# The third graph layer, too, does its first 256 destinations by fetching the rows of single edges

## The chip, the cores and the metric

The kernel runs on one core of a Trainium2 chip. The metric is the device time of one execution in microseconds. Before the change, three timed executions gave 1886.87, 1888.71 and 1895.72 us; the median is 1888.71 us.

## The reference: what is computed

There are 3125 nodes with 256 features each, and 103125 edges (50000 random pairs in both directions and one loop per node), sorted by destination. Four blocks follow each other, each with a layer norm ahead of it and a residual sum behind it: a graph attention network of three layers, a mixture of 16 experts (two per node), a graph sum layer, and a mixture of 8 experts (one per node). The change concerns the three attention layers, and the way in which the rows of the third go on to the 16 experts:

```
def _gat_layer(x, src, dst, W, al, ar, b, n_nodes):
    h = x @ W
    el = h @ al
    er = h @ ar
    e = jax.nn.leaky_relu(el[src] + er[dst], 0.2)
    m = jax.ops.segment_max(e, dst, num_segments=n_nodes)
    ex = jnp.exp(e - m[dst])
    s = jax.ops.segment_sum(ex, dst, num_segments=n_nodes)
    alpha = ex / s[dst]
    return jax.ops.segment_sum(alpha[:, None] * h[src], dst, num_segments=n_nodes) + b

h = relu(_gat_layer(layernorm(x), src, dst, W1, al1, ar1, b1, n))
h = relu(_gat_layer(h, src, dst, W2, al2, ar2, b2, n))
x = x + _gat_layer(h, src, dst, W3, al3, ar3, b3, n)
```

## The kernel before

**Tiles and groups.** Nodes lie in 25 tiles of 128 (the last has 53). Destinations are done in 13 groups: twelve of 256 (two tiles) and one of 53. A matrix of edge counts, source by destination, is kept on the chip as bytes; the first layer builds it on the way. The exponential of the leaky score is written as a product and a maximum, so that a group needs, for each of the 25 source tiles (a *step*), one DVE instruction and two products on PE. The DVE instruction (L1388) makes `pm` = max(tau, rho) x counts, 128 sources by 256 destinations. The products (L1391) multiply its two halves with the sources' rows `h` (256 features and a column of weights, 257 columns) and accumulate in PSUM. A float32 product stands in the profile as two records, so a step has four and a group 100. Six `pm` buffers let DVE run ahead of PE. `terms` (L1277, L1280) makes tau of the next group in the middle of a group.

**What follows a group.** During the next group, `divide` (L1428 to L1437) divides by the weights and adds the bias. In layers one and two, the "onward" steps then turn the tile (L1289), multiply it with the next layer's weights (L1161) and keep rows, scores and exponentials (L1168 to L1172). In layer three, the router takes over (`Router.group`): `norm` (L616 to L621), `gate` (L629 to L639), and `send` (L241 to L249 and L644 to L677). `send` picks two experts per node, finds each row's place by a running count `pre` (PE at L661 and L662) and scatters two rows per node to HBM with an indirect DMA on POOL's queue (L677), four per group. POOL also adds the bias to the residual input `y` (L1359) and writes node numbers and weights into the rows (L675, L676).

**The rows apart (class `Apart`).** In layer two, the first four tiles (512 destinations) are not done by products. As layer one ends, every source row with its weights (258 numbers) is saved to HBM by a DMA on SP's queue. In layer two POOL then fetches single rows by indirect DMA (L1933), one destination per partition: 38 edges for each tile (`OWN`), and beforehand 20 more (`HEAVY`) for the at most 128 destinations of all four tiles that have more than 38 edges. Each fetch of 128 rows is one *slot*. Four slots make a batch, and five batches of buffers make a ring. DVE makes the coefficients of a batch (`apart_co`, L1950) and adds up each slot (`apart_acc`, L1957 and L1959). The sums of the heavy destinations are brought back to their places by a product with a transposed one-hot matrix (L1964; the matrix is made in `begin`, L1875 to L1914). `EVERY`, `LANDED` and `STEP` say after how many steps of the layer each batch, slot and fetch stands in the program; a fetch into the ring stands behind the last slot of the batch whose buffer it takes.

**What sets the order.** Layer two is issued as written (`manual_schedule`). Layers one and three are ordered by the scheduler of the tile framework, which places instructions by its own estimates. Each engine works through its queue in order, so an instruction that waits holds all those behind it. In layer two, ten groups (2 to 11) and the short last one are left. In layer three, all 13 are done by products, and the first of them starts its sources at tile 4, since the tiles done apart come last (`of`).

**The write of empty rows.** `spare_rows` clears parts of the HBM buffers by 34 DMAs on SP's queue, one in every eighth step from the third group of layer one on.

Of the kernel before, what the change touches and what calls it, by code (L numbers as in the profile page):

```python
# [10 lines left out]
F32 = mybir.dt.float32  # L11
# [6 lines left out]
OP = mybir.AluOpType  # L18
# [4 lines left out]
P = 128  # L23
# [543 lines left out]
class Router:  # L567
# [6 lines left out]
    def __init__(self, tc, cp, ident, eps, iota, count, rows, sums, gate_w, gate_b, table):  # L574
# [3 lines left out]
        self.before, self.every = count  # L578
        self.gw = cp.tile([P, KD, NX0], F32, name="gate_w")
# [25 lines left out]
    def group(self, wp, rp, pp, x, t0, n):  # L605
# [35 lines left out]
        def send():  # L641
# [16 lines left out]
            for i, t in enumerate(tiles):  # L658
                nc.vector.tensor_tensor(self.pre[:, t + 1], self.pre[:, t], sel[:, i], op=OP.add)
            rank = pp.tile([P, n, NX0], F32, name="ps_z")  # L660
            nc.tensor.matmul(rank, self.before, sel, start=True, stop=False)  # L661
            nc.tensor.matmul(rank, self.every, self.pre[:, t0:t0 + n], start=False, stop=True)  # L662
# [420 lines left out]
APART = 2  # L1083
FEW = 2 * APART
OWN = 38
HEAVY = 20
SLOTS_OF = [(FEW, HEAVY)] + [(t, OWN) for t in range(FEW)]
BATCH_OF = 4
BATCHES_OF = [(t, k, min(BATCH_OF, n - k)) for t, n in SLOTS_OF for k in range(0, n, BATCH_OF)]
RING = 5  # L1090
LANDED = 19.0
FETCH = 11
BEGIN = 0
RANK = [(5, 0), (5, 4), (5, 6), (5, 9), (5, 14), (5, 17), (6, 8)]
EVERY = 1.31
STEP, LAST_STEP = 0.976, 0.25
# [78 lines left out]
def dense_attention(tc, dram, counts, x_in, big, ident, eps, layers, src, dst, rows, high, make_router, over, count):  # L1175
# [10 lines left out]
    with tc.tile_pool(name="dw", bufs=1) as cp, tc.tile_pool(name="dwl", bufs=2) as wl, \  # L1186
# [3 lines left out]
        with tc.tile_pool(name="dp", bufs=6) as pmp, tc.tile_pool(name="ds", bufs=2) as sp, \  # L1190
# [92 lines left out]
            def onward_steps(at, y, t, r, name, nxt, w, save):  # L1283
# [15 lines left out]
                def keep():  # L1299
                    nxt.keep(t, r, held["ps"])  # L1300
                    if save:
                        save.save(nxt, t, r)
# [6 lines left out]
            raws, soon = [None], []  # L1309
            fills = []  # L1310
            for i in range(3):
                last = i == 2
                bt_i = bt
                if last:
# [6 lines left out]
                    nxt, we_n = None, None  # L1321
                else:
                    nxt = Sources(tc, big, small)
                    we_n, bt, products = attention_weights(tc, wl, cp, layers, i + 1, now.rho[:, NT - 1:])
                    products()
                apart_now, now_apart = i == 1, []
                if apart_now:
                    hold = ExitStack()
                    hp = hold.enter_context(tc.tile_pool(name="hp", bufs=1))
                    raws[0] = hp  # L1330
                    hq = hold.enter_context(tc.tile_pool(name="hq", bufs=1, space=PSUM))
                    def finished(t, acc, b=bt_i, nxt=nxt, w=we_n):
                        col = hp.tile([P, 1], F32, name="apart_col", bufs=2)
                        nc.vector.tensor_scalar(col, acc[:, D:], 1e-30, None, op0=OP.max)
                        nc.vector.reciprocal(col, col)
                        nc.vector.scalar_tensor_tensor(acc[:, :D], acc[:, :D], col, b, op0=OP.mult, op1=OP.add)
# [5 lines left out]
                if apart_now:  # L1342
                    order.enter_context(tc.manual_schedule())
# [788 lines left out]
```

## Time and profile before the change

| what | value |
|---|---|
| timed runs, median (lowest to highest) | 1888.71 us (1886.87 to 1895.72) |
| the profiled execution, its own time | 1840.01 us |
| its span, first to last instruction | 1838.2 us |
| mean granted clock of PE | 0.990 |
| layer one, first to last product L1391 | 67.8 to 443.8 us |
| layer two | about 453 to 726 us |
| layer three | about 727 to 1021 us |
| from the end of layer three to the first expert's products | 1021 to 1042.9 us |

The profile has a page of totals and groups of instructions ("line engine op, out<-in xcount | busy us, mean ns | idle before, and what ended it"), a list of waits ("who waited for whom: us in total, times, longest"), busy times by window, and timelines ("start, length, engine, line, operation; in brackets the idle time just before it and what ended it"). Line numbers are those of the kernel before. A busy PE says little on its own, since products overlap; the pace of its records and what it waits for say more. Lengths on DVE overlap too: two of them in a row can start closer together than one of them lasts.

### The profile page before, as it was taken

The page shows a single profiled execution, that of the slowest core. Times are in us where ns is not written, and L with a number is a line of the kernel's source. Part 1 is how long each engine was busy: PE and PEld are TensorE (multiplying, and loading weights), DVE is VectorE, ACT ScalarE, POOL GpSimd, SP SyncE. Part 2 cuts the span into 40 slices and gives each one's busy share as a digit, 9 for nine tenths or more (in the row PEclk, how much of TensorE's full clock was granted, in tenths as well). Part 3 has the DMA queues.
Part 4 walks back from the last instruction along what each step waited for, and adds up shares of the span by engine and source line. Part 5 has one row for each costly group of instructions (what it writes and reads, how often), then busy time and mean ns, then how long its engine had stood idle before and what let it go on. Part 6 is the DMA issues. An engine that isn't in the chain of part 4 may idle for free. (4 is left out here: it accounts for less than half of the span.)

```text
span 1838.2 us, 27323 instructions
## 1 busy us (share of the span) xinstructions
PE 1771.2 (96%) x9249; PEld 1389.5 (76%) x9249; DVE 1017.4 (55%) x2865; ACT 725.4 (39%) x2078; POOL 501.5 (27%) x636
## 2 busy tenths in 40 slices
PE   5999999999999999999999799999989999999997
PEld 4788888887887886888888466666668886555886
DVE  6888888875777887777777422222262222233221
ACT  3767667671111111222222211111148998444221
POOL 5210110000677774223322233333200000222221
PEclk9999999999999999999999899999999999999999
DMA  4111213757333332211111576776330002624664
GB/s 118 33 48 47 67 64 139 298 236 312 80 93 95 98 93 78 62 46 40 40 44 37 178 196 196 204 217 168 66 82 1 1 1 74 225 115 166 215 203 127
DMA packets 118370, 211.50 MB, mean 115 GB/s; under 512 B 14843, under 2 KB 80929, under 8 KB 118184
## 3 DMA queue, kind: packets, MB, share of 16 engines
q1 hardware_dynamic: 78228, 130.30, 20.9%
q0 software_dynamic: 24848, 56.84, 11.8%
q10 hardware_dynamic: 15138, 22.44, 3.7%
q8 instruction: 79, 1.29, 0.3%
q14 instruction: 77, 0.63, 0.1%
HBM read 118.61 MB, written 93.00 MB: 115 GB/s over the span
## 5 line engine op out<-in xcount | busy, mean ns | idle before, releaser
L1391 PE MATMUL acc<-big,pm 128*128 128x257 f32 x3400 | 787.7, 383 | 8.9 <-DVE pm L1388 8.9
L1391 PEld LDWEIGHTS acc<-big,pm 128*128 128x128 f32 x3400 | 628.6, 190 | 99.4 <-DVE pm L1388 15.4
L1388 DVE SCALAR_TENSOR_TENSOR pm<-tau,big,counts 128x256 f32<-128x256 f32 x850 | 398.3, 487 | 99.9 <-PE acc L1391 96.0
L1933 POOL DMA_INDIRECT apart_row<-apart_rows,apart_who x172 | 186.7, 1085 | 62.6 <-issue 39.3
L775 PE MATMUL ps_h<-xsT,w 128*128 128x384 f32 x512 | 168.4, 487 | 0.6 <-ACT xsT L751 0.6
L1543 PE MATMUL acc<-msg,cr 128*128 128x512 f32 (+1 forms) x625 | 157.9, 403 | 0.0
L775 PEld LDWEIGHTS ps_h<-xsT,w 128*128 128x128 f32 x512 | 96.7, 190 | 66.9 <-issue 1.9
L1543 PEld LDWEIGHTS acc<-msg,cr 128*128 128x128 f32 (+1 forms) x625 | 114.7, 185 | 29.2 <-ACT cr L1539 1.2
L1539 ACT ACTIVATE cr<-counts 128x256 fp32r<-128x256 uint8 (+1 forms) x325 | 130.6, 402 | 14.2 <-PE acc L1543 7.0
L1799 ACT CAST counts<-acc_c 128x500 uint8<-128x500 f32 (+1 forms) x155 | 95.9, 677 | 94.8 <-PE acc_c L1789 94.7
L1024 PE MATMUL ps_y<-t_wd,hsT 128*128 x480 | 108.8, 380 | 0.4 <-ACT hsT L1052 0.4
L1774 DVE TENSOR_TENSOR ohk<-iota_k,key 128x2016 f16<-128x2016 f16 (+1 forms) x79 | 94.6, 1197 | 19.8 <-PE acc_c L1789 19.7
L778 ACT ACTIVATE silu<-ps_h 128x384 f32<-128x384 f32 x64 | 31.4, 490 | 182.2 <-PE ps_h L775 182.1
L795 POOL DMA_INDIRECT sums<-y,who x48 | 74.7, 1556 | 85.9 <-DVE y L793 73.0
L1024 PEld LDWEIGHTS ps_y<-t_wd,hsT 128*128 128x128 f32 x480 | 88.8, 190 | 11.6 <-ACT hsT L1052 0.6
L779 DVE TENSOR_TENSOR hid<-silu,ps_h 128x384 f32<-128x384 f32 x64 | 35.2, 553 | 108.7 <-PE ps_h L775 103.9
L1768 ACT ACTIVATE ohs<-iota_s,low 128x128 f16<-128x128 f16 x286 | 94.1, 400 | 0.0
L930 PE MATMUL ps_H<-big,t_w 128*128 128x512 f32 (+1 forms) x224 | 93.1, 552 | 0.8 <-ACT H L932 0.5
L790 PE MATMUL ps_o<-w,hid 128*128 128x256 f32 x384 | 87.2, 379 | 0.0
L1789 PEld LDWEIGHTS <-ohs 128*128 128x128 f16 x1250 | 77.7, 98 | 10.9
L1789 PE MATMUL acc_c<-ohk,ohs 128*128 128x125 f16 x1250 | 84.5, 218 | 0.0
L1959 DVE SCALAR_TENSOR_TENSOR apart_acc<-apart_row,apart_co,apart_acc 128x257 f32<-128x257 f32 x167 | 80.9, 485 | 1.6
(380 smaller groups left out, 2073.5 us busy)
## 6 DMA issues: line engine op xcount, KB each, us to landing
rows<-empty SPq DMA_DIRECT2D x16, 2564.0 KB, 15.7
w<-in_L_ffn_w_dram ACTq DMA_DIRECT2D x42, 512.0 KB, 4.9
hs<-rows SPq DMA_DIRECT2D x29, 641.0 KB, 4.4
big<-in_L_ffn_w_dram SPq DMA_DIRECT2D x30, 512.0 KB, 9.2
rows<-empty SPq DMA_DIRECT2D x16, 516.0 KB, 4.8
t_wd<-in_L_ffn_Wd_dram SPq DMA_DIRECT2D x8, 1024.0 KB, 10.7
xs<-rows SPq DMA_DIRECT2D x15, 387.0 KB, 3.4
bias<-in_L_ffn_bd_dram SPq DMA_DIRECT2D x30, 128.0 KB, 4.0
```

Of the source, the lines that this page charges most:

```text
L775: nc.tensor.matmul(ps, w[:, k, j * P:(j + 1) * P], xsT[:, k], start=(k == 0), stop=(k == KD - 1))
L930: nc.tensor.matmul(ps[:, :n], a[:, k, j * P:(j + 1) * P], xnT[:, k, c:c + n], start=(k == 0), stop=(k == KD - 1))
L1024: nc.tensor.matmul(ps, hsT[:, j], d[:, ds(e, 1), j, :].rearrange("p o f -> p (o f)"), start=(j == 0), stop=(j == nh - 1))
L1388: nc.vector.scalar_tensor_tensor(pm[:, :n], tau[:, :n], now.rho[:, of:of + 1], edges[:, of, :n], op0=OP.max, op1=OP.mult)
L1391: nc.tensor.matmul(acc[:r, j, :D + 1], pm[:, q:q + r], now.h[:, of, :D + 1], start=(s == 0), stop=(s == NT - 1))
L1539: nc.scalar.activation(cr[:, :n], edges[:, s, :n], AF.Copy, accum_out=seen[:, a * NT + s:a * NT + s + 1])
L1543: nc.tensor.matmul(acc[:r, j].rearrange("p h d -> p (h d)"), cr[:, q:q + r], msg[:, s].rearrange("p h d -> p (h d)"), start=(s == 0), stop ...
L1768: nc.scalar.activation(far[:, i], self.iota_s, AF.Abs, scale=-1.0, bias=self.low32[:, batch, i:i + 1])
L1774: nc.vector.tensor_tensor(to[:, i:tiles].rearrange("p t (x u) -> p t x u", u=2), iota.rearrange("p (x u) -> p x u", u=2)[:, None].to_broad ...
L1789: nc.tensor.matmul(acc[:, u], ohs[:, i], ohk[:, i, :KEYS], start=(t == 0), stop=(t == TW - 1))
L1799: nc.scalar.copy(to[:, :, d0 % PAIR:d0 % PAIR + whole * WIN].rearrange("p s (u d) -> p u s d", u=whole), acc[:, :whole])
L1933: nc.gpsimd.indirect_dma_start(out=row[:, j], out_offset=None, in_=self.table[:, :], in_offset=bass.IndirectOffsetOnAxis(ap=self.who[:, q ...
```

## The change

- `SKIP = [0, 2, 1]`: layer two skips its first two groups as before, and layer three now skips its first group (tiles 0 and 1), which is done by row fetches: 20 heavy slots and 2 x 38, 96 in all, in 25 batches.
- As layer two goes on, its rows are saved to a second table in HBM.
- The ring of layer three has three batches; its slots are planned from 22 us on, one in every 1.9 steps (`EVERY`), against 1.31 us in layer two. What both layers need (row numbers, the transposed one-hot matrix, which slots are real) is kept over both (`stay`).
- Layer three is still ordered by the scheduler, but `pinned` fixes the order of all `pm`, `apart_co` and `apart_acc` instructions on DVE among themselves, as written. The product that brings back the heavy sums takes its PSUM tile from the common pool `ps_m` (two buffers) and holds it until its tile is done.
- The residual input of tiles 0 and 1 is loaded into `y_out` directly; when tile 1 is done, its routing is put into the current group's steps 15, 17 and 20 (or the next group's). The running count `pre` goes by the order of sending (`sent`) and no longer by tile number.
- `begin` moves from step 0 to step 11, just ahead of the first fetches, in both layers.
- After the last group of layer two, the onward steps come five steps earlier, as they did after layer one.
- The writes of empty rows come in every sixth step; their buffer lies in memory that layer one gives back.

```diff
--- before.py
+++ after.py
@@ Router.send
-            for i, t in enumerate(tiles):
-                nc.vector.tensor_tensor(self.pre[:, t + 1], self.pre[:, t], sel[:, i], op=OP.add)
+            k = self.sent
+            self.sent += n
+            for i in range(n):
+                nc.vector.tensor_tensor(self.pre[:, k + i + 1], self.pre[:, k + i], sel[:, i], op=OP.add)
...
@@ constants
-APART = 2
-FEW = 2 * APART
+SKIP = [0, 2, 1]
+FEW = 4
-RING = 5
-LANDED = 19.0
-BEGIN = 0
-EVERY = 1.31
-STEP, LAST_STEP = 0.976, 0.25
+RING = [0, 5, 3]
+LANDED = [0.0, 19.0, 22.0]
+EVERY = [0.0, 1.31, 1.9]
+STEP = [0.0, 0.976, 1.0]
+LAST_STEP = 0.25
@@ dense_attention
-                apart_now, now_apart = i == 1, []
+                apart_now, now_apart, fixed = SKIP[i] > 0, [], i == 1
+                if apart_now and not stays:
+                    stays.append(tc.tile_pool(name="hk", bufs=1))
+                    apart.stay(third.enter_context(stays[0]), pp)
...
+                    if fixed:
+                        hq = hold.enter_context(tc.tile_pool(name="hq", bufs=1, space=PSUM))
+
+                    def finished(t, acc, b=bt_i, nxt=nxt, w=we_n, i=i, hp=hp):
                         col = hp.tile([P, 1], F32, name="apart_col", bufs=2)
...
+                        to, add = (acc[:, :D], b) if i < 2 else (y_out[:, t], y_out[:, t])
+                        apart.pinned(lambda: nc.vector.scalar_tensor_tensor(to, acc[:, :D], col, add, op0=OP.mult,
+                                                                            op1=OP.add))
+                        if i < 2:
+                            soon.extend(onward_steps(now_step[0] + 1, lambda: acc, t, P, "yT1", nxt, w,
+                                                     lambda *of: apart.save(of[0], i + 1, *of[1:])))
+                        elif t % 2:
+                            steps = router.group(wp, rp, zp, y_out, t - 1, 2)
+                            start = now_step[0] + 1
+                            start += max(0, 15 - start % NT) if start % NT < 18 else NT + 15 - start % NT
+                            soon.extend(zip((start, start + 2, start + 5), steps))
+
+                    now_apart += apart.events(i, hq, finished)
+                    if last:
+                        for t in range(2 * SKIP[i]):
+                            nc.sync.dma_start(y_out[:, t], x_in[t * P:(t + 1) * P])
+                            nc.gpsimd.tensor_tensor(y_out[:, t], y_out[:, t], bt_i, op=OP.add)
                 order = ExitStack()
-                if apart_now:
+                if fixed:
                     order.enter_context(tc.manual_schedule())
+                apart.last = [] if apart_now and not fixed else None
                 for a, (c, n) in enumerate(GROUPS):
-                    if apart_now and a < APART:
+                    if a < SKIP[i]:
                         continue
...
-                            of = (s + FEW) % NT if last and a == 0 else s
+                            of = (s + (2 * SKIP[i - 1] if i and a == SKIP[i] else 0)) % NT
...
-                        if apart_now and (a, s) == (APART, BEGIN):
-                            apart.begin(hp, hq, pp, now.lr)
-                        if apart_now and (a, s) == (APART, FETCH):
-                            for b in range(RING):
-                                apart.fetch(b)
+                        if apart_now and (a, s) == (SKIP[i], FETCH):
+                            apart.begin(i, hp, pp, now.lr)
...
-                        if s % 8 == 2 and fills:
+                        if s % 6 == 2 and fills:
                             fills.pop(0)()
...
-                    sooner = 2 if a == len(GROUPS) - 2 else 5 if i == 0 and a == len(GROUPS) - 1 else 0
+                    sooner = 2 if a == len(GROUPS) - 2 else 5 if not last and a == len(GROUPS) - 1 else 0
...
-                            if save:
-                                apart.save(nxt, t, r)
+                            apart.save(nxt, i + 1, t, r)
...
@@ Apart
+    def pinned(self, what):
+        if self.last is None:
+            return what()
+        with self.tc.issue_after(self.last[0]) if self.last else ExitStack():
+            made = what()
+        self.last[:] = [made.ins]
+        return made
...
+    def begin(self, i, hp, pp, lr):
+        nc = self.nc
+        self.hp, self.pp, self.i = hp, pp, i
+        few = 2 * SKIP[i]
...
+        self.batches = [(t, k, min(BATCH_OF, self.span(t)[1] - k)) for t in [FEW] + list(range(few))
+                        for k in range(0, self.span(t)[1], BATCH_OF)]
+        for b in range(RING[i]):
+            self.fetch(b)
...
         def at(q):
-            time, whole = LANDED + EVERY * q, STEP * NT * (len(GROUPS) - 1 - APART)
-            return math.ceil(time / STEP if time < whole else whole / STEP + (time - whole) / LAST_STEP)
+            time, whole = LANDED[i] + EVERY[i] * q, STEP[i] * NT * (len(GROUPS) - 1 - SKIP[i])
+            return math.ceil(time / STEP[i] if time < whole else whole / STEP[i] + (time - whole) / LAST_STEP)
...
         def expand(t):
-            ps = state["ps"] = self.hq.tile([P, D + 1], F32, name="apart_ps")
+            ps = state["ps"] = hq.tile([P, D + 1], F32, name="apart_ps") if hq else \
+                self.pp.tile([P, D + 1], F32, name="ps_m")
             nc.tensor.matmul(ps, self.back[:, t], state["heavy"], start=True, stop=True)
```

## The prediction

> **What bounds the kernel now.** I read the totals, then the stages by window, then the waits of PE in the second and third graph layer, then timelines inside those layers.
>
> ```profile
> PE 1771.2 (96%) x9249; PEld 1389.5 (76%) x9249; DVE 1017.4 (55%) x2865; ACT 725.4 (39%) x2078; POOL 501.5 (27%) x636
> ...
> L1391 PE MATMUL acc<-big,pm 128*128 128x257 f32 x3400 | 787.7, 383 | 8.9 <-DVE pm L1388 8.9
> ...
> L1388 DVE SCALAR_TENSOR_TENSOR pm<-tau,big,counts 128x256 f32<-128x256 f32 x850 | 398.3, 487 | 99.9 <-PE acc L1391 96.0
> L1933 POOL DMA_INDIRECT apart_row<-apart_rows,apart_who x172 | 186.7, 1085 | 62.6 <-issue 39.3
> ```
>
> PE is the bound (96%), and L1391, the edge product of the graph layers, is its largest part: 34 groups of 25 steps, 100 records each. DVE waits for PE (96.0 us), not PE for DVE (8.9 us). POOL's 27% is an average: its 172 row fetches all lie in layer two.
>
> Two windows, cut at the first divide (L1428) of a group: eight groups of layer two, ten of layer three. Columns: busy us and count of PE, PEld, DVE, ACT, POOL; clock; DMA share; GB/s.
>
> ```profile
> 484.44:692.84 208.40, 202.97 (x951) 173.32 (x949) 165.10 (x452) 29.81 (x103) 162.86 (x150) 1.00 0.36 95
> 751.17:989.33 238.16, 235.85 (x1161) 204.40 (x1161) 179.33 (x631) 51.11 (x100) 73.51 (x144) 1.00 0.16 49
> ```
>
> A group of layer three takes 238.16/10 = 23.82 us, 0.953 a step, with PE 99% busy: whatever PE is spared here is won. DVE is at 75% already, since the routing of finished rows runs here; POOL is at 31%.
>
> The waits of PE in these two windows (total, times, longest):
>
> ```profile
> PE acc L1391 <- DVE pm L1388: 5.0, 8, 1.1
> ```
>
> ```profile
> PE ps_z L661 <- DVE g_sel L657: 2.3, 10, 0.2
> ```
>
> In layer two, which already fetches rows, PE lost at least 5.0 us: pm late, because DVE stood at apart_co for a row. In layer three PE waits once per group, 0.23 us, for the routing chain on DVE. That chain has no slack left.
>
> The fetches in layer two and the products in layer three, in order of time (start, length; in brackets the idle time):
>
> ```profile
> 566.53 0.96 POOL L1933 DMA_INDIRECT apart_row<-apart_rows,apart_who  x1 [0.30 <-issue]
> 567.79 0.96 POOL L1933 DMA_INDIRECT apart_row<-apart_rows,apart_who  x1 [0.30 <-DVE apart_acc L1959]
> ```
>
> ```profile
> 810.83 0.18 DVE L639 TENSOR_TENSOR g_z<-ps_z,gate_b 128x32 f32<-128x32 f32 x1
> ...
> 815.38 0.19 DVE L657 TENSOR_TENSOR g_sel<-g_both,real 128x32 bf16<-128x32 f32 x1
> 815.49 0.48 DVE L1388 SCALAR_TENSOR_TENSOR pm<-tau,big,counts 128x256 f32<-128x256 f32 x1
> 815.89 0.36 DVE L659 TENSOR_TENSOR pre<-pre,g_sel 128x16 bf16<-128x16 bf16 x2
> ```
>
> ```profile
> 816.21 15.43 PE L1391 MATMUL acc<-big,pm 128*128 128x257 f32 x70
> ```
>
> A fetch costs POOL 1.26 us start to start at best. First to last, 172 of them took (708.2-470.4)/171 = 1.39 us each: POOL worked without rest. A pm keeps DVE 0.40 us (815.49 to 815.89), although its record lasts 0.48. PE needs (15.43-0.38)/69 = 0.218 us a record.
>
> **What the Trainium skill says.** "DMA: Bandwidth & Descriptors", section "SWDGE vs HWDGE vs iDMA": DMAs issued from GpSimd have their descriptors made by a program on its cores. The trace agrees: 0.96 us of POOL per fetch, and the row lands 2.9 us (median) after issue. "Perfetto Trace Analysis", "GPSIMD Engine Instruction": spans there are unreliable, use start-to-start spacing; hence 1.39 and not the mean of 1.085. "SBUF — State Buffer", "SBUF: two separate sides": GpSimd and VectorE share one port pair as an exclusive lock, taken by a DVE instruction with two SBUF inputs when the GpSimd operation reads SBUF. Each added slot is such an instruction. The trace fits: one pm took 2.05 us at 708.84 while POOL added y (L1359).
>
> **The change, part by part.**
>
> *Removed.* One group of layer three: 100 records x 0.218 = 21.8 us, and its two tau transposes, 0.22 us (573.55 to 573.77): **-22.0 us** on PE, which is the path. On DVE, 25 pm go.
>
> *Added on PE.* Per layer the heavy rows' tau: 8 small records, 455.89 to 456.81, 0.92 us. Two products L1964 that spread the heavy sums, 0.43 us each (592.76 to 593.19). **+1.8 us.** The transposed hot matrix is kept from layer two.
>
> *Added on POOL.* 96 fetches (20 + 2 x 38) beside its own work in layer three: 7.35 us per group (73.51/10) plus 0.30 us ahead of each of four row scatters, 8.55 us. The plan places one slot per 1.9 steps, 1.81 us; POOL needs 1.39 for the fetch and 8.55 x 1.9/25 = 0.65 for its other work, 2.04. Short by 0.23 us a slot. The first 12 rows fill the ring beforehand; for the other 84 that is 19.0 us. Against it stands a lead: fetching starts at step 11 (10.5 us), ends its first 12 and two y additions at about 29, and gets the first free buffers then (their slots are due at step 36; DVE is about five steps ahead of PE, 4.5 us). The next four land at about 38 and are due at step 53, 46 us: 7.7 us to spare. So the last rows come some **11 us late**. Layer two is the yardstick. PE's work in a group there is 100 x 0.218, two tiles onward at 1.09 (489.17 to 490.26 is a transposition, 0.22; four records 0.87) and tau 0.22, 24.2 us, and the apart tiles add some 5 us in eight groups: 198.6, where they took 208.4. So 9.8 us were lost. One slot per 1.31/0.976 = 1.34 steps of 0.993 us is 1.33 us against 1.39: short by 0.057 us, 9.8 us over 172. So PE loses nearly all of the shortage; what six pm buffers cover is small.
>
> *Added on DVE.* Per group 13.2 slots x 0.40 and 3.3 apart_co x 0.25 = 6.1 us. DVE's idle time is 5.9 us per group ((238.16-179.33)/10), and closing up 25 pm (0.48 to 0.40) frees 2.0 more: it fits by under 2 us. Not in the chain from g_z to g_sel, 4.7 us: the built order of the changed program puts three slots, one apart_co and one more pm into it, 1.85 us, while PE gets about 1.5 steps (1.3 us) more to do before it asks. PE's wait thus grows by about 0.6 us in seven and a half groups, 4.6 us. Queued behind the waiting apart_co are the pm's and the routing, because the new pins fix the order of slots and pm's on DVE; for them waits PE. This is not added to POOL's 11: while PE stands at the chain, POOL catches up. I take **+10 us** for both; ends 2 (fetches at 1.26: POOL needs 1.91, short by 8 us, covered by the lead; half of the chain) and 28.
>
> *Moved or free.* Routing of tiles 0 and 1: same instructions, at step 215 instead of the second group; the slots end at step 207, so DVE has room. Its scatters pass POOL's fetches when these are over. The saving of layer two's rows: 25 SP stores of 129 KB, 2.4 us each to land, 3.2 MB in 260 us beside 95 GB/s: hidden by DMA being 36% busy; if not, rows land later, up to 2 us. The last save must land before the first fetch; layer two's last group goes on five steps sooner, so both meet near step 11. begin in layer two moves from step 0 to 11: its 0.78 us wait for ACT may go or stay, taken as 0. The clearing writes in layer one come every sixth step: 2564 KB per 7.6 us (a step there is 1.21 us: the divides of two groups start at 266.87 and 297.08) is 337 GB/s, above the 312 of the busiest slice, but PE waits for no DMA there, and the gathers among them (5.6 us to land at most) are used 16 steps, 19 us, later. 0, else 3 us. Expert weights whose memory the ring now holds load later in the layer, not needed before 1042. The held ps_m buffer (expand to gather, 23 steps) sees one tau transpose, for which the other buffer is there: 0.
>
> Sum: -22.0 + 1.8 + 10 = **-10.2 us**. Of the profiled execution (1840.0, span 1838.2) that leaves 1829.8. The timed runs have a median of 1888.7, 2.6% more, which this profile doesn't account for; I carry the difference over unscaled: **1878.5 us**. If every PE step there is 2.6% longer, POOL gets 5 us more and the gain is up to 5 us larger.
>
> **The rivals.**
> 1. *The fetches are covered.* For: the fetch's median of 0.965 us, and DMA only 16% busy in layer three. Then only the chain is left: -22.0 + 1.8 + 4.6 = -15.6, **1873**.
> 2. *The gain is used up.* POOL's queue is served in order, and stands at g_wt, g_to and y loads (97.4, 2.4 and 18.7 us of waiting in ten groups now). If 0.4 us a group of that stays, with fetches queued behind (3 us), and lateness and chain add up, 11 + 4.6 + 3 = 18.6; -1.6, **1887**. Against: a late POOL finds them done.
> 3. *DVE's order becomes the bound: slower.* Place: the chain from g_z to g_sel. Each late row holds the pm's and the routing behind it, and PE then stands at ps_z with pm's already made, so its six buffers are of no use. It decides from (22.0-1.8)/7.5 = 2.7 us lost per group. With the 11 us of lateness paid, and the five slots and one apart_co that stand between g_z and g_to paid in full as well (2.25 us in each of 7.5 groups, 17), the loss is 28, 3.7 us per group: +7.8, **1896.5**. Against: DVE's average load fits.
>
> **The numbers.** Forecast 0.40 (own range 1874 to 1883), rival one 0.27, two 0.20, three 0.13. Leaving out half of the third and the tip of the first gives 1868 to 1893. Faster or slower by over 0.5% (9.4 us, about what a measurement of this kernel tells from no change): faster means below 1879.3; rival one and two thirds of the forecast, 0.53; same 0.34; slower 0.13.
>
> **What would show it.** After the change: L1391's successor with 3300 records; layer three's groups at 23.8 us before and after the slots, 25 or more among them; POOL nearly always busy there; DVE waiting at apart_co for DMA; PE's wait for g_sel near 0.9 us. Wrong if groups stay at 23.8 throughout (rival one), if they pass 26.5 (three), or if layer one or two moved by over 3 us.

## The result, and the profile after

The changed kernel takes 1898.62 us (median of 20 runs), the kernel before 1887.51 us beside it (20 runs): ratio 1.005, 95% interval 1.0031 to 1.0069. It is slower by half a per cent. 1878.5 us was forecast, with a range from 1868 to 1893. The profiled execution took 1894.2 us (span 1892.5).

One thing has to be known before any number here is read. The kernel before has two speeds, by session (a stretch of runs made together): in some sessions all its runs take 1833 to 1846 us, in others 1878 to 1907. The profile of before (1840) is of the first kind, here called A. Its timed runs and all runs of the result are of the second, B. The chip numbered 2 was seen in both kinds, so it isn't a matter of the chip's number. What makes a session A or B was not found. Ratios are always taken within one session.

The totals of the changed kernel's page (a session B). Columns: busy us, share, records; for groups, busy us, mean ns, idle time before.

```profile
PE 1776.3 (94%) x9159; PEld 1381.7 (73%) x9159; DVE 1044.0 (55%) x2969; ACT 724.3 (38%) x2079; POOL 588.9 (31%) x726
...
L1412 PE MATMUL acc<-big,pm 128*128 128x257 f32 x3300 | 784.5, 388 | 27.6 <-DVE pm L1408 15.2
...
L1408 DVE SCALAR_TENSOR_TENSOR pm<-tau,big,counts 128x256 f32<-128x256 f32 x825 | 385.0, 486 | 121.0 <-PE acc L1412 92.6
L1974 POOL DMA_INDIRECT apart_row<-apart_rows,apart_who x268 | 274.9, 1026 | 145.3 <-issue 68.6
```

The work is what was forecast: 3300 records of L1412 (before: L1391, 3400) and 96 more fetches. But PE's idle time ahead of L1412 rose from 8.9 to 27.6 us. The stages tell where. Eight groups of layer two, then eight of layer three, cut at first divides; same columns as in the prediction:

```profile
493.79:738.42 244.63, 213.55 (x934) 177.90 (x934) 165.28 (x453) 29.81 (x103) 152.53 (x149) 0.93 0.36 91
802.66:1016.15 213.49, 196.90 (x935) 166.20 (x934) 187.25 (x660) 44.77 (x89) 150.60 (x202) 0.96 0.35 101
```

Layer three's groups take 213.49/8 = 26.7 us where 23.8 were before. Layer two's take 30.6, where the profile of before had 26.05, though its groups are unchanged but for the saves. PE's granted clock, 1.00 in both windows before, is 0.93 and 0.96.

PE's waits in the first window, and in the second (total, times, longest):

```profile
PE acc L1412 <- DVE pm L1408: 13.1, 7, 4.9
PE ps_m L1162 <- ACT yT L1292: 10.4, 2, 8.5
PE acc L1412 <- issue: 8.8, 8, 5.2
PE ps_m L1162 <- issue: 4.1, 1, 4.1
```

```profile
PE ps_z L664 <- DVE g_sel L658: 10.2, 6, 3.4
PE ps_x L635 <- DVE row L630: 5.3, 2, 4.3
```

In layer three the wait for g_sel is at the place that the prediction named, the end of the routing chain on DVE: 10.2 us in eight groups, where ten groups had 2.3. Another 5.3 us come at an earlier step of the routing (`row`), which the prediction did not name. In layer two 36.4 us, before 5.0, come in 18 waits of up to 8.5 us. One of them in order of time, PE, POOL and ACT:

```profile
556.64 0.38 PE L1290 MATMUL ps_m<-ident,y 128*128 128x128 f32 x2
556.86 1.03 PE L1412 MATMUL acc<-big,pm 128*128 128x257 f32 x4
...
560.46 0.96 POOL L1974 DMA_INDIRECT apart_row<-apart_rows,apart_who  x1 [0.30 <-issue]
561.51 0.38 ACT L1292 ACTIVATE yT<-ps_m 128x256 f32<-128x256 f32 x1 [20.57 <-remote]
561.72 0.95 POOL L1974 DMA_INDIRECT apart_row<-apart_rows,apart_who  x1 [0.30 <-issue]
...
561.95 2.09 PE L1162 MATMUL ps_m<-we,yT 128*128 128x258 f32 x4 [4.05 <-issue]
```

The transposition ended at 557.02. ACT, free for 20 us, needs only that, and begins at 561.51. "Remote" means that the word of PE's end came so late that the profile no longer ties it to PE's instruction. DVE stood still from 558.08 to 566.10, and from 558.08 to 561.51 POOL alone worked, fetching. So either PE's work or PE's *signal* is late (the ends of PE's instructions are modelled in a profile).

The trace decides, since it also keeps the times at which a semaphore was raised, the signal that ends a wait. PE's products and transpositions signal by one semaphore. It was raised at 559.99, 561.44, 561.49 and 563.57, though no instruction of PE that raises it ended between 557.89 and 564.03; and ACT began 0.02 us after the raise at 561.49. It is the signal that is late. Raises of PE's semaphore over 0.5 us after the last end of such an instruction, counted over whole layers (the runs e1 to e15 follow below; the traces of kind B lack up to 18% of these raises, those of kind A next to none):

| run | session | late raises in layer two | late raises in layer three |
|---|---|---|---|
| before | A | 0 of 302 | 0 of 370 |
| before again (e1) | B | 51 of 263, up to 11.3 us | 2 of 359, up to 0.7 us |
| changed | B | 59 of 271, up to 8.1 us | 17 of 278, up to 2.8 us |
| changed again (e9) | A | 0 of 310 | 0 of 339 |
| paced unread fetches (e10) | A | 0 of 302 | 0 of 371 |
| paced unread fetches (e13) | B | 61 of 258, up to 5.8 us | 44 of 322, up to 2.6 us |
| no fetches (e15) | B | 0 of 363 | 2 of 361, up to 0.6 us |

Late signals stand in sessions of kind B, and there nearly all in the layers that fetch rows.

### The profile page after: what moved, and what is told of

It reads as the page before. It is cut to its first block, busy times and chain, and to the rows that moved or that the text cites. A ratio compares the mean times of both kernels' runs of the same rounds, so it can differ in the third digit from the quotient of the medians.

```text
span 1892.5 us, 27417 instructions
## 1 busy us (share of the span) xinstructions
PE 1776.3 (94%) x9159; PEld 1381.7 (73%) x9159; DVE 1044.0 (55%) x2969; ACT 724.3 (38%) x2079; POOL 588.9 (31%) x726
## 3 DMA queue, kind: packets, MB, share of 16 engines
q8 instruction: 77, 1.26, 0.3%
## 5 line engine op out<-in xcount | busy, mean ns | idle before, releaser
L1412 PE MATMUL acc<-big,pm 128*128 128x257 f32 x3300 | 784.5, 388 | 27.6 <-DVE pm L1408 15.2
L1412 PEld LDWEIGHTS acc<-big,pm 128*128 128x128 f32 x3300 | 616.7, 193 | 124.7 <-DVE pm L1408 23.3
L1408 DVE SCALAR_TENSOR_TENSOR pm<-tau,big,counts 128x256 f32<-128x256 f32 x825 | 385.0, 486 | 121.0 <-PE acc L1412 92.6
L1974 POOL DMA_INDIRECT apart_row<-apart_rows,apart_who x268 | 274.9, 1026 | 145.3 <-issue 68.6
L2001 DVE SCALAR_TENSOR_TENSOR apart_acc<-apart_row,apart_co,apart_acc 128x257 f32<-128x257 f32 x260 | 127.5, 490 | 1.9
L1292 ACT ACTIVATE yT<-ps_m 128x256 f32<-128x256 f32 (+1 forms) x25 | 9.5, 378 | 216.0 <-PE ps_m L1290 148.3
L1162 PE MATMUL ps_m<-we,yT 128*128 128x258 f32 (+1 forms) x248 | 71.6, 409 | 16.0 <-ACT yT L1292 10.4
```

Source lines behind the costliest of these rows:

```text
L1408: apart.pinned(lambda: nc.vector.scalar_tensor_tensor(pm[:, :n], tau[:, :n], now.rho[:, of:of + 1], edges[:, of, :n], op0=OP.max, op1=OP.m ...
L1412: nc.tensor.matmul(acc[:r, j, :D + 1], pm[:, q:q + r], now.h[:, of, :D + 1], start=(s == 0), stop=(s == NT - 1))
L1974: nc.gpsimd.indirect_dma_start(out=row[:, j], out_offset=None, in_=self.tables[self.i][:, :], in_offset=bass.IndirectOffsetOnAxis(ap=self. ...
L2001: self.pinned(lambda: nc.vector.scalar_tensor_tensor(state["acc"], row[:, j, :D + 1], co[:, j:j + 1], state["acc"], op0=OP.mult, op1=OP.add))
```

## The experiments

"Layer two" and "layer three" are the times between the starts of `col<-acc,col` (L1426 before, L1445 after) in the last, short groups of the layers; "rest" is from there to the end of the span. One profiled execution each, in us:

| run | session | end of layer 1 | layer two | layer three | rest | timed ratio to before |
|---|---|---|---|---|---|---|
| before | A | 458.0 | 271.1 | 292.1 | 817.0 | |
| before again (e1) | B | 462.1 | 332.5 | 292.4 | 818.8 | 0.9994 |
| changed | B | 454.0 | 319.7 | 298.3 | 820.5 | 1.005 |
| changed again (e4) | B | 457.7 | 329.2 | 303.9 | 821.2 | |
| changed again (e9) | A | 456.4 | 266.5 | 284.9 | 819.7 | 0.9962 |
| layer three by products (e2) | B | 454.1 | 321.9 | 293.2 | 820.7 | 1.0017 |
| no saves (e3) | B | 458.9 | 318.2 | 300.6 | 1048.5 | 1.1252 |
| slower slots (e7) | A | 457.0 | 266.7 | 276.5 | 821.3 | 0.9922 |
| ring of three (e8) | A | 457.5 | 264.4 | 284.1 | 820.8 | 0.9953 |
| both sizes (e11) | A | 460.0 | 268.2 | 277.9 | 819.6 | 0.9905 |
| both sizes (e14) | B | 457.4 | 331.2 | 306.9 | 819.4 | 1.0103 |
| paced unread fetches (e10) | A | 460.9 | 268.4 | 292.2 | 816.7 | 0.9995 |
| paced unread fetches (e13) | B | 458.4 | 322.6 | 307.5 | 814.8 | 1.0096 |
| no fetches (e12) | A | 455.9 | 300.2 | 293.1 | 820.3 | 1.0172 |
| no fetches (e15) | B | 457.4 | 300.2 | 293.4 | 820.2 | 0.9872 |

In sessions of kind A layer two took 266.9 to 272.8 us in the profiles whose layer two is that of before, so a difference of a few us there tells nothing.

**Before again, and three more beside it (e1 to e4).** My first theory ("theory A" below; theories and kinds of session share letters): the stops go with row fetches, in any kernel; rivals: the saves of layer two's rows (theory B), or the forecast's own late rows (theory C).

> The kernel before, unchanged, for a second profile. Seen so far: in the profile of the changed kernel DVE and PE stand still together for 3 to 8 us several times in layers two and three while POOL goes on fetching, and the PE clock is halved for some 7 us after most of them; the profile of before had almost none of that, and it is 48 us shorter than the median of its own timed runs. Theory A (the stops go with the row fetches, in any kernel): this profile is near 1885 us, not 1840, its clock near 0.973, its layer two takes 300 to 325 us instead of 273, and its layer three, which fetches nothing, stays at 23.8 us a group. Theory B (the stops come from the saves of layer two's rows, which only the changed kernel has): layer two takes 273 to 280 us again, and the 48 us are elsewhere. Theory C (the forecast's: POOL late and the routing chain on DVE, in layer three alone): as B for this run.

> The changed kernel with SKIP = [0, 2, 0]: layer three computes all its destinations by products again and layer two saves no rows; the other edits of the change stay. The result is the same function. Theory A: all that is lost by the change comes with the 96 added fetches, so the time is that of before, 1885 to 1890 (ratio 0.998 to 1.002), layer three at 23.8 us a group without stops, layer two as in the run of before. Theory B: 1885 to 1890 as well, but layer two without the stops that the changed kernel shows. Theory C: 1885 to 1890. If instead one of the side edits (clearing writes at every sixth step, begin at step 11, the last group of layer two five steps sooner) is what costs, the time stays at 1893 or more.

> The changed kernel without the saves of layer two's rows: layer three fetches its rows from the table of layer one's, so that its first 256 destinations are computed from the wrong layer's rows; the work is otherwise the same. Theory A: 1895 to 1900, as the changed kernel, stops of the same length in layers two and three. Theory B: stops in layer two vanish, and the time falls by 20 us or more, to 1850 to 1878. Theory C: as the changed kernel, or up to 2 us less.

> The changed kernel again, for a second profile. Theory A: stops of DVE and PE in layers two and three again, but at other places than in the first profile, since they hang on chance meetings of a fetch with DVE's or PE's work; layer two 300 to 325 us, layer three's groups 23.5 to 31 us in disorder. Theory B: stops in layer two at the same places, beside the saves. Theory C: layer three's groups of 25 us while rows are added, evenly, and the stops of the first profile gone.

e2 is `SKIP = [0, 2, 0]`. e3 changes two lines of the changed kernel:

```
-        if SKIP[i]:
+        if SKIP[i] and i < 2:
             self.nc.sync.dma_start(self.tables[i][t * P:t * P + r], sources.h[:r, t])
...
-                out=row[:, j], out_offset=None, in_=self.tables[self.i][:, :],
+                out=row[:, j], out_offset=None, in_=self.tables[1][:, :],
```

Measured, medians: e1 1892.29 (before beside it 1890.87), e2 1894.68 (ratio 1.0002 to 1.0033), e3 2128.41, e4 1913.67 (one run, 1.2% over before). The kernel before, run beside them, has the stops too; eight groups of layer two and ten of layer three in e1:

```profile
492.50:756.40 263.90, 212.25 (x922) 176.68 (x922) 164.45 (x452) 29.74 (x103) 165.04 (x156) 0.90 0.29 78
816.70:1054.80 238.10, 235.80 (x1161) 204.36 (x1161) 179.72 (x631) 51.19 (x100) 72.95 (x144) 1.00 0.16 49
```

263.90 us for the eight groups that took 208.40 in the first profile, and 238.10 for layer three's ten, as ever (238.16): the layer that fetches loses 55 us, the layer that doesn't loses none. (This profiled execution took 1907.5 us, 15 more than the median of e1.) Theory B falls: e1 has no saves of layer two, and e3, without them, has the stops (318.2). e3's total tells nothing: the wrong rows route the nodes otherwise, and its extra time lies in the rest. e2 shows no stops in layer three; its 0.4 to 6.2 us over before are the price of the change's other edits in a session B.

**Fetches that nobody reads, additions on POOL, and two sizes (e5 to e8).** This was a session A (before 1838.15).

> The kernel before, with 96 row fetches added to POOL in layer three, one at every second step from step 29 on, into eight buffers that nothing reads; no products are removed and DVE gets no slots. Theory A, sharpened by the second profiles: the fetches themselves delay the completion signals between PE, ACT and DVE. In the trace of the first profile of e1 PE's transposition ended at 602.5 and ACT, which waited for nothing else, began at 612.6; layer two takes 319 to 332 us in four profiles where the free profile of before took 271, some 0.3 us lost per fetch. Then layer three here grows by 15 to 30 us with stops of PE, and the time is 1905 to 1920. Theory D (the loss in layer three is the slots on DVE and the rows that come late, not the fetch): layer three stays at 292 to 295 us and the time at 1889 to 1893.

> The kernel before, with 96 additions of 128x256 on POOL in layer three, at the steps where the run with the unread fetches has its fetches; their result is not used. POOL is busy for about as long (0.8 us each) and reads and writes the SBUF, but makes no descriptors and starts no DMA. Theory A: no stops, 1888 to 1893. If it is POOL's use of the SBUF, shared with VectorE, that stops the others, this run shows stops or longer DVE instructions and gets slower as much as the unread fetches do (10 us or more). Theory D: 1889 to 1895.

> The changed kernel with the slots of layer three at every 2.2 steps in place of 1.9, so that POOL's 2.04 us per slot fit into 2.2 us. Theory D and the forecast's own sum: rows are no longer late, the waits at apart_co go, layer three's groups fall by about 1.3 us (11 us over the layer), time 1885 to 1892. Theory A: the same 96 fetches delay the same signals, only spread thinner; 1893 to 1900, layer three 295 to 303 us.

> The changed kernel with three buffers of four rows in layer two in place of five. Theory A: while signals are late DVE stands still, and POOL goes on until it has no free buffer; the late signals then get through. Twelve rows instead of twenty ahead end a stop some 8 us earlier, so layer two's 320 to 330 us fall to 295 to 315, unless rows then come late. Theory D, or rows that need the lead: layer two gets longer by 10 us or more, time above 1905.

e7 is `EVERY = [0.0, 1.31, 2.2]`, e8 is `RING = [0, 3, 3]`. e5 and e6 add to the kernel before:

```
+ k = (a * NT + s - 29) // 2
+ if last and (a * NT + s - 29) % 2 == 0 and 0 <= k < 96:
+     nc.gpsimd.indirect_dma_start(out=un.tile([P, ROW], F32, name="unread", bufs=8), out_offset=None,
+         in_=apart.table[:, :], in_offset=bass.IndirectOffsetOnAxis(ap=apart.who[:, k:k + 1], axis=0))
```

(e6: `nc.gpsimd.tensor_tensor(un, un, bt_i, op=OP.add)`.) e5 took 1917.55 us (1.0426) and e6 1891.54 (1.029), but both experiments failed as designed. Nothing tied the new instructions to the steps, so the scheduler put them far ahead in POOL's queue; PE then waited 77.1 us in one piece in e5 for what stood behind them. They price a wrong order of a queue, not a fetch.

e7 took 1823.12 (0.9909 to 0.9935) and e8 1829.38 (0.9941 to 0.9965). So in a session A the changed kernel, at these sizes, is faster than before. With slower slots layer three takes 276.5 us; whether that is a gain over the changed kernel itself, e9 tells.

**The same question in both kinds of session (e9 to e15).** When these expectations were written I took the two kinds for kinds of chip; read "session" for "chip" in them. Theory A2: in a session B each fetch costs more than in a session A, because it delays completion signals. Theory D: the loss is late rows and the routing chain alone, whatever the session.

> The changed kernel once more, beside the kernel before on the same chip. The runs so far fall into two kinds by chip: on one chip the kernel before takes 1838 us, as its first profile, on others 1887 to 1891, as its timed runs. Theory A2: on a chip of the second kind completion signals come late beside row fetches, which costs some 0.3 us per fetch, so that 96 more of them use up the 20 us that PE is spared: +8 to +12 us there. On a chip of the first kind there is no such delay, and the change does what the forecast's sum said for the profile of 1840: -8 to -12 us, 1826 to 1830. Theory D (late rows and the routing chain, whatever the chip): the same difference from before on either kind.

> The kernel before, with 96 row fetches added in layer three that nothing reads, but tied to the steps this time: DVE writes one column of each buffer (128x1) after every second step's pm, and the fetch into it waits for that. (In the earlier run POOL took them far ahead of the steps and then stood before the additions to y, so that PE was idle for some 80 us: that run told of the order of a queue, not of the price of a fetch.) Theory A2: on a chip where before takes 1838, layer three stays within 5 us and the time at 1838 to 1845; where it takes 1890, each fetch costs some 0.3 us: layer three grows by 20 to 30 us, time 1908 to 1920. Theory D: +2 to +8 us on either, since POOL's scatters of routed rows get later behind the fetches.

> The changed kernel with both sizes changed: slots of layer three at every 2.2 steps, and three buffers of four rows in layer two. Each alone gave 1823 and 1829 on the chip where before takes 1838. Theory A2: there, 1820 to 1826. On a chip where before takes 1890: the shorter lead bounds how long POOL can go on while signals are late, layer two 300 to 318 us; 1870 to 1892. Theory D: 1870 to 1880 there, as its gain over the changed kernel (6 us or more) does not depend on the chip.

> The changed kernel with SKIP = [0, 0, 0]: no layer fetches rows, all destinations of all layers are computed by products; the same function. Layer two then has two more groups of products, 50 us of PE work at 25 us a group, and no fetches. Theory A2: on a chip where before takes 1838, 1855 to 1875. Where before takes 1890, layer two falls from 320-332 to 290-300 us, without stops, and the time is 1850 to 1872: fetching costs more there than it spares. Theory D (fetching pays in layer two on any chip): 1905 or more there.

These four ran in a session A (before 1839.9). Three of them ran again in a session B (before 1894.5), on a chip of the same number:

> The kernel before with 96 unread row fetches in layer three, tied to the steps, as in the run that gave +0 us on a chip where before takes 1840. Theory A2, if the chip is one where before takes 1890: each fetch costs some 0.3 us, layer three grows from 292 to 310-322 us with stops of PE, ratio 1.010 to 1.016. Theory E (on such a chip it is not the fetch that is slow but DVE's and PE's dependence on rows that come late: the unread rows hold nobody up): layer three 292 to 298 us, ratio 0.999 to 1.004. If the chip is of the faster kind, both say 0.998 to 1.002.

> The changed kernel with slots at every 2.2 steps in layer three and three buffers in layer two, which gave 0.9905 of before on a chip where that takes 1840. Theory A2, if the chip is one where before takes 1890: the fetches are as many as in the changed kernel, so most of the loss stays; the shorter lead ends each stop sooner. Ratio 0.990 to 1.001, layer two 295 to 318 us. Theory E: layer three is late no more, so the gain over the changed kernel is that of the faster kind (0.6%) or larger: ratio 0.990 to 0.999.

> No fetches in any layer, which gave 1.017 of before on a chip where that takes 1840. Theory A2 and theory E, if the chip is one where before takes 1890: the stops go with the fetches, layer two takes 298 to 302 us as it did there (300), layer three 293, and the time is 1868 to 1876 on this chip too: ratio 0.988 to 0.993, faster than before and than the changed kernel. If something else on such a chip is slow (the clock, the DMA queues of layer one, the expert layers), the time is above 1900.

e10 and e13 tie each unread fetch of e5 to its step, by one small write on DVE (59 ns; `made` is the pm of the step):

```
+ unread = un.tile([P, ROW], F32, name="unread", bufs=8)
+ with tc.issue_after(made.ins):
+     nc.vector.memset(unread[:, 0:1], 0.0)
+ nc.gpsimd.indirect_dma_start(out=unread, ...)
```

e11 and e14 have both sizes of e7 and e8. e12 and e15 have `SKIP = [0, 0, 0]`, and a pool of their own for the buffers that the ring's pool held.

Session A, medians and intervals: e9 1832.82 (0.9949 to 0.9976), e10 1839.79 (0.9985 to 1.0005), e11 1822.21 (0.9890 to 0.9920), e12 1871.36 (1.0157 to 1.0187). Session B: e13 1908.82 (1.0061 to 1.0130), e14 1916.5 (1.0078 to 1.0128), e15 1872.45 (0.9848 to 0.9897).

The pair e10 and e13 decides: one program, nothing read, nothing removed. Ten groups of layer three, in e10 and in e13:

```profile
751.40:989.70 238.30, 235.89 (x1161) 204.42 (x1161) 186.12 (x727) 51.57 (x100) 167.00 (x240) 1.00 0.37 104
```

```profile
803.10:1056.30 253.20, 241.50 (x1162) 203.96 (x1161) 182.84 (x726) 51.08 (x100) 170.48 (x240) 0.99 0.34 98
```

In A, 96 fetches beside the products cost nothing: POOL busy for 167 of 238 us, DMA more than doubled from 0.16, PE still 99% busy. In B the same fetches lengthen the groups by 14.9 us; the timed runs say 18 (0.0096 x 1894.5; by the interval 12 to 25), some 0.19 us per fetch (0.12 to 0.26). That is a little less than theory A2 had forecast (1.010 to 1.016). Theory D falls for the sign of the result, and so does theory E, which let only rows that somebody waits for cost anything. And without fetches the two kinds of session are equal: e12 and e15 differ by 1.1 us, and layer two takes the same in both:

```profile
455.94:756.10 300.16, 299.32 (x1428) 255.72 (x1427) 159.42 (x395) 40.14 (x140) 2.58 (x6) 1.00 0.01 2
```

```profile
457.39:757.55 300.16, 299.31 (x1428) 255.72 (x1427) 159.46 (x395) 40.09 (x140) 2.56 (x6) 1.00 0.01 2
```

What makes a session B slow therefore needs fetches to show.

e14 went against me: in B the shorter ring and slower slots don't bound the loss, but stand at 1.0103, above the changed kernel's 1.005 (of another session). The idea that a stop ends when POOL runs out of buffers is not borne out: layer two took 331.2 us with three buffers and 319.7 and 329.2 with five. Nor is there one price per fetch: e11's gain of 17.7 us in A, less e13's 18, would leave e14 where before is, and it lost 19.5 us (14.8 to 24.3). Between profiles of the same program in A and in B, a fetch of layer three costs 0.14 to 0.30 us and one of layer two 0.31 to 0.37.

**Which part of a fetch? (e16 to e18)**

> The kernel before with 96 unread loads of 128 rows in layer three, tied to the steps as the 96 unread fetches were, but plain loads issued by SP: the same 132 KB each, rows in a row, no descriptors made by POOL. Theory F (what delays the others is the fetch's making on POOL, not its bytes): in a session where before takes 1890, ratio 0.998 to 1.003. Theory G (it is the bytes that pass the DMA engines into the SBUF): 1.006 to 1.013, as the fetches (1.0096). Where before takes 1840: 0.999 to 1.001 by both.

> The kernel before with 96 additions of 128x256 on POOL in layer three, tied to the steps (DVE clears the 128x256 that POOL adds to); no DMA. The first run of this kind was not tied to the steps and told nothing of this. Theories F and G: 0.998 to 1.004 in either kind of session, DVE's clearing being some 0.15 us in time that it has. If POOL's use of the SBUF holds up DVE: slower by 0.5% or more in both kinds.

> As the loads by SP, but issued by POOL: its program makes the descriptors, yet of a plain load and not of a gather by an index per row. Theory F: in a session where before takes 1890, 1.003 to 1.012, in between or as the fetches. Theory G: 1.006 to 1.013. If only the gather matters (an index read per row, a descriptor per row): 0.998 to 1.003. Where before takes 1840: 0.999 to 1.001.

They are e10 with the fetch replaced by `nc.sync.dma_start(unread, apart.table[k * 31:k * 31 + P])`, by an addition on POOL into `unread` (which DVE clears, 128x256), and by the plain load on `nc.gpsimd`. It was a session A (before 1837.44), so F and G are not told apart. e16: 1838.84 (0.9995 to 1.0018), e18: 1837.74 (0.9994 to 1.0015). e17: 1850.01 (1.0052 to 1.0088), slower; its layer three took 304.1 us. DVE's `pm` in layer three, between 751 and 940 us, in e17 and then in e10 (busy us, mean ns, idle before):

```profile
L1389 DVE SCALAR_TENSOR_TENSOR pm<-tau,big,counts 128x256 f32<-128x256 f32 x186 | 111.1, 608 | 6.5 <-PE acc L1392 4.7
```

```profile
L1389 DVE SCALAR_TENSOR_TENSOR pm<-tau,big,counts 128x256 f32<-128x256 f32 x199 | 103.7, 527 | 34.5 <-PE acc L1392 32.2 <-ACT tau L1280 1.4
```

96 additions lengthen a pm to 608 ns; 96 fetches to 527, from 495 in the kernel before. "SBUF — State Buffer", section "SBUF: two separate sides", which the prediction used, has GpSimd (POOL) and VectorE (DVE) share a lock on one port pair. The additions agree with it; the fetches hardly touch it. Part of e17's loss is DVE's own clearing, though (272 ns each, 25 us of DVE time in that stretch), and the two were not separated.

## Why the prediction was wrong, point by point

*The step that failed.* "The timed runs have a median of 1888.7, 2.6% more, which this profile doesn't account for; I carry the difference over unscaled: 1878.5." The difference is of -10.2 us, and its sign holds for the kind of session that the profile shows: there the changed kernel measures 0.9962 of before, -7.1 us, and its profiled execution of 1829.4 us stands beside the forecast's 1829.8. The unexplained 48.7 us were not a cost that both kernels bear alike. They lay in layer two (332.5 us in e1's profile, for 271.1), with its 172 fetches: some 0.3 us for each by the timed runs. A change that adds 96 fetches adds to them, since PE's signals come late beside fetches (in e13's layer three 44 of 322). With e13's price for layer three, -7.1 + 18 = +11 us, and +0.5% of 1887.5 (5.9 to 13.0 us) was measured. That this sum comes out so well is luck, since the same sum fails for e14 by 19 us; the sign and the rough size of the cost are shown, a fixed price is not.

*Products removed, -22.0, and added, +1.8.* These fit: in e7, where DVE no longer waits for rows, layer three falls by 15.6 us against before (292.1 to 276.5). That is rival one's sum (-15.6) to the decimal, which leaves its 4.6 us for the chain. The agreement to a tenth is luck: five waits for g_sel remain in eight groups of e7, 4.6 us in all, but 0.23 us per group of that was there before, so the chain grew by some 2.8.

*POOL and the chain, +10.* In A layer three's groups lengthen among the slots, as forecast: eight of them took 25.7 us each in e9, with DVE 91% busy.

```profile
746.83:952.20 205.37, 193.40 (x947) 165.69 (x946) 187.19 (x660) 44.83 (x89) 149.69 (x204) 0.98 0.37 106
```

The whole layer: 284.9 - 292.1 = -7.2 us against -20.2 for the products alone, so 13.0 us. 4.6 of them stay in e7; 8.4 its slower slots take away, with DVE's waits for rows (5.9 us in e9). So rows were late for want of POOL's time (2.04 us per slot against 1.81 planned), and its 11 us of lateness were near. The place, too, is that of the forecast. In the changed kernel's first profile (a session B):

```profile
863.40 0.22 DVE L1991 SCALAR_TENSOR_TENSOR apart_co<-apart_row,apart_tau,apart_real 128x4 f32<-128x4 f32 x1 [3.45 <-DMA apart_row<-apart_rows,apart_who]
864.86 0.18 DVE L640 TENSOR_TENSOR g_z<-ps_z,gate_b 128x32 f32<-128x32 f32 x1
...
871.94 0.18 DVE L658 TENSOR_TENSOR g_sel<-g_both,real 128x32 bf16<-128x32 f32 x1
```

DVE stands 3.45 us for a late row, the chain from g_z to g_sel takes 7.3 us (before 4.7), and PE waits 3.43 us for it. "This is not added to POOL's 11" was too hopeful: both were paid.

*What the sum lacked: the clock.* "TensorE: Matmul & The Clock Gate", section "Part 1: The HAM clock gate (the "warmup" mystery)", says that PE's clock falls to half after an idle window of some 3.4 us, and rises after a busy one. The trace agrees on the half. It differs on the idle time: here the clock fell at 870.91, 2.2 us after PE's stop, and stayed down for 6.8 us. Around that wait (busy us and count of PE; clock; DMA share; GB/s):

```profile
864.00:868.00 4.00, 4.00 (x21) 1.00 0.38 98
868.00:872.00 4.00, 0.75 (x4) 0.86 0.14 36
872.00:876.00 4.00, 3.82 (x10) 0.50 0.37 99
876.00:880.00 4.00, 4.00 (x16) 0.78 0.36 95
```

PE stopped from 868.75 to 872.18, and the products after it ran at half clock: (0.14 + 0.50 + 0.22) x 4 = 3.4 us of clock lost, 0.6 of it while PE stood. So this wait of 3.4 us was paid nearly twice. Over the span, the mean clock is 0.976 where the profile of before had 0.990: (1 - 0.976) x 1892.5 - (1 - 0.990) x 1838.2 = 27 us of PE time, of which some fell in idle time. The prediction priced waits by their length alone.

*Moved or free.* Saves: no cost found (e3 has 318.2 us in layer two without them). begin and the seam to layer two: from the divide of its last full group to its end, layer one took 14.1 us in e10 (446.8 to 460.9) and 10.6 in e9 (445.8 to 456.4); the forecast had 0. The rest of the kernel: some +3 us in every version of the changed kernel but e3, with fetches in layer three or without (820 for 817); in e9 PE waits 2.9 us for the first expert's rows (L753), before 0.4. Why they come later was not looked into. The two errors cancel.

*Layer two as yardstick.* "So 9.8 us were lost" was true of the kind of session that the profile shows, and not of the timed runs to which the forecast was applied: there layer two lost some 50 us more. The yardstick made the rate at which a late POOL is paid (nearly one for one) look known. In A it held roughly.

*The rivals.* Three had the right sign and the right place (DVE's chain), at 3.7 us per group; 26.7 - 23.8 = 2.9 was found, in B, above the 2.7 from which it was to decide. But in A, with the same order on DVE, the gain stays. So DVE's order alone doesn't make the change slower: late signals, and the clock that falls after long stops, come on top. That rival three's 1896.5 lies 2 us from the measured 1898.6 is therefore luck.

*What stays open.* What differs between the sessions, and which part of a fetch delays the signals (bytes, descriptors, or the gather; e16 and e18 met only a session A). Late raises are seen of PE's semaphore alone; of DVE's and ACT's, the traces of kind B lack 15 to 29% in the layers that fetch, so nothing is known of those. Kind B leaves one mark without fetches, too: of the raises of eight DMA semaphores, e12's trace keeps 353 to 371 each, e15's 237 to 347. No run took the delay away except by taking the fetches away.

*A version that beats both* depends on the session. In A, both sizes (e11), 0.9905. In B, no fetches at all (e15), 0.9872, though it loses 1.7% in A. None won in both.

## What to carry to other kernels

When the profile's own execution is some per cent shorter than the timed runs, find out first what the longer ones do in that time, and profile the old kernel again: what is missing from the profile may scale with just the thing that the change adds. Price a stop of PE of some us by its length and by the half clock that can follow it. Where an engine begins late and nothing seems to hold it, compare the times at which its semaphore was raised with the ends of the instructions that raise it. And measure a change that trades PE work for fetches in more than one session before believing either sign.

## What was not expected of the hardware

- The same program with 172 row fetches takes 1838 us in one session and 1891 in another; with none, 1871.36 and 1872.45.
- In a session B an engine can begin 4 to 10 us after the end of the only instruction that it waits for, while POOL makes fetches every 1.26 us. In e1, PE's transposition ended at 602.53 us and ACT began at 612.58. PE's last instruction before that ended at 603.41, yet its semaphore was still raised at 605.42, 608.27, 610.44 and 612.55.
- 96 fetches paced over 184 us cost PE nothing in a session A (0.9995), while 96 additions of 128x256 on POOL, with DVE's clearing, cost 12.6 us.
